# Perceiver block, expert slots: rows read six slots ahead and ahead of the weights; latent weights queued after the gathered rows

## The chip, the core and the metric

The kernel runs on one core of one Trainium2 chip. The metric is device time in microseconds (us) of that core. Three runs of the kernel before gave 1575.37, 1575.95 and 1579.69 us; the median is 1575.95 us.

## What is computed

Eight batches of 64 latent rows of 512 (512 rows in all) pass through two layers; each attends to a context of 8 x 1601 x 512. Everything is float32. Cut to what matters here:

```python
x = x + cross_attention_16_heads(layernorm(x), ctx, ...)        # layer 0
x = x + gated_scan(layernorm(x), ...)
x = x + ffn(layernorm(x), router_w, router_b, expert_w, expert_b)
#   ffn: each row goes to the one expert of 8 with the largest probability:
#   y = gate * (row @ expert_w[idx] + expert_b[idx])
x = x + cross_attention_1_head(ctx, ctx, layernorm(x), ...)     # layer 1
x = x + latent_attention(layernorm(x), Wq, Wl, Wk, Wv, Wo, ...)
x = x + encoder_layer_with_moe(layernorm(x), ..., w1, w2, ...)
```

The change touches the expert ffn of layer 0 and the loading of the weights of latent_attention (Wq 512x512, Wl 512x128, Wk and Wv 128x512, Wo 512x512) in layer 1.

## The kernel before, in words

**Layer 0 and routing.** The 512 rows lie in four tiles of 128. A tile is routed (`route_tile`, `places`), and its normalised rows are scattered to an array in DRAM, `xsd`, by an indirect transfer that GpSimd issues (L985). `xsd` has 11 slots of 128 rows (E + MORE = 8 + 3): one for each expert, and three that are given to experts with more than 128 rows.

**Expert slots** (`slots()`, L1127 to L1189). For each slot s, the rows `xs[s]` are read from `xsd` (`rows`, L1145, 256 KB), TensorE turns them (`turn`, L1149 and L239, result `xsT`), eight matmul instructions multiply them by the expert weights `ws[s]` (`fetch`, L1136 or, for the slots 8 to 10, an indirect transfer issued by GpSimd at L1139; 1 MB), VectorE copies the result to `ys` (L1165), and it is written to `ysd` in DRAM (L1166, 256 KB). Weights have four buffers (WE = 4), so the weights of slot s + 4 are asked for when slot s has been multiplied; before the change the rows of slot s + 4 are asked for just after them. Slot s + 2 is turned after slot s is multiplied. At slot 6 the third piece of the context of the first two batches is asked for as well (`context(0, 2)`, L1247, four tiles of 512 KB).

After slot 10, GpSimd gathers each token's row out of `ysd` (tiles `g`, L1180, four transfers of 256 KB), VectorE adds it to x (L1182) and normalises (L104 to L109, with two steps on GpSimd at L98 and L99), TensorE turns the result and makes the queries of the layer 1 attention (`queries1`).

**Layer 1.** `scores1` multiplies queries by the transposed context (tiles `w` from `ctxT`, bank `psc`), `attend1` multiplies probabilities by the context (tiles `w` from `ctx`, bank `pa`), both for pairs of batches bp = 0 to 3, in chunks c = 0 to 2 of four tiles of 512 KB each and a short tail. These tiles come out of a ring of 14 buffers (`ring_tile`): a tile can be asked for when TensorE is through with the one 14 before it. `latent_weights()` (L1290), called by the first `attend1`, asks for the five transfers of the latent weights (L1293: `lwq` 1 MB, `wl` 256 KB, two halves of `wkv` 256 KB each, `lwo` 1 MB) and six rows of biases (L1079). `latent(t)` uses them later. The last stage, the encoder layer with its own experts, streams 64 MB of weights (`w1`, `w2`).

**What sets the order.** Nearly all loads and stores are issued by SyncE (SP), one after another in a fixed order: one that has to wait holds up all that are behind it. An SP transfer can wait for a buffer, for the data that it reads, and for one of eight earlier transfers to land, so that at most eight are in flight. TensorE's order is written out in the program (`interleave`, and a manual schedule). For SP the order is written out by hand up to the end of `slots()` (`in_order.close()`, L1186); behind that a scheduler places the transfers, and `tc.keep_in_program_order` keeps a step from being moved ahead of where the program has it.

Of the kernel before, what the change touches and what calls it, by code (L numbers as in the profile page):

```python
# [16 lines left out]
NT = 4  # L17
DC = 4
SK = 1601
E, FF, CAP = 8, 2048, 64  # L20
WE = 4
MORE = 3
SLOTS = E + MORE
CH = [(0, 512), (512, 512), (1024, 512), (1536, 65)]
# [21 lines left out]
def perceiver_kernel(ctx: ExitStack, tc: tile.TileContext, a: dict, out: bass.AP):  # L46
    nc = tc.nc
# [7 lines left out]
    def name(s):  # L55
        count[0] += 1
        return f"{s}_{count[0]}"

    def ps(tag, shape=(128, 512), bufs=None):
        n = name(tag)  # L60
        return pools["psum"].tile(list(shape), F32, tag=tag, name=n, bufs=bufs)
# [39 lines left out]
    def layer_norm(dst, src, g=None, b=None):  # L101

        st = sm([128, 6], "ln_st")
        nc.vector.bn_stats(st, src)  # L104
        mv = sm([128, 2], "ln_mv")
        nc.vector.bn_aggr(mv, st)
        rs = sm([128, 1], "ln_rs")
        rsqrt(rs, mv[:, 1:2])
        nc.vector.tensor_scalar(dst, src, mv[:, 0:1], rs, ALU.subtract, ALU.mult)  # L109
        if g is not None:  # L110
            nc.vector.tensor_mul(dst, dst, g)
            nc.vector.tensor_add(dst, dst, b)
# [120 lines left out]
    def mm(p, w, m, start=True, stop=True, share=1.0):  # L233
        nc.tensor.matmul(p, w, m, start=start, stop=stop)  # L234
        n = m.free_size()
        clock[0] += share * max(2 * 0.85 * n, 230.0)
# [121 lines left out]
    posi = small.tile([128, NT], mybir.dt.int32, tag="posi", name="posi", bufs=1)  # L358
    wrow = small.tile([128, MORE], mybir.dt.int32, tag="wrow", name="wrow", bufs=1)
    xsd, ysd = [tc.dram_tile((SLOTS * 128, D), F32, name=nm) for nm in ("xsd", "ysd")]  # L360


    with ExitStack() as st:
# [588 lines left out]
        def places():  # L952
# [31 lines left out]
            for t in range(NT):  # L984
# [6 lines left out]

            past = work[:, 128 : 128 + MORE * E].rearrange("p (s e) -> p s e", e=E)
            nc.vector.tensor_tensor(
                past, upto.unsqueeze(1).to_broadcast([128, MORE, E]),
                iota0[:, :MORE].unsqueeze(2).to_broadcast([128, MORE, E]), ALU.is_le,
            )
            whose = work[:, 256 : 256 + MORE]
            nc.vector.reduce_sum(whose, past, axis=AX.X)
# [70 lines left out]
    routed = ctx.enter_context(ExitStack())  # L1069
    we = routed.enter_context(tc.tile_pool(name="we", bufs=WE, reuse_waits="tile"))  # L1070

# [5 lines left out]
    def row(nm, pool=None, bufs=3):  # L1077
        r = (pool or md).tile([128, D], F32, tag="row", name=name("row"), bufs=bufs)
        nc.sync.dma_start(r, a["rows"][ROWS.index(nm)].partition_broadcast(128))  # L1079
        return r  # L1080
# [4 lines left out]
    def t2(nm):  # L1085
        return md.tile([128, D], F32, tag="t2", name=name(nm), bufs=14)
# [27 lines left out]
    def flip_tile(v):  # L1114
        p = ps("pt")
        for c in range(DC):
            flip(p[:, ts(c, 128)], v[:, ts(c, 128)])
        return p
# [4 lines left out]
    x_mid = [Event() for _ in range(NT)]  # L1123
    x_out = [Event() for _ in range(NT)]
    xns, probs1 = {}, {}

    def slots():  # L1127


        ws, xs, xsT = first_ws, {}, {}  # L1130

        def fetch(s):
            if s < E:
                if s > 1:
                    ws[s] = we_tile(s)
                nc.sync.dma_start(ws[s], table[ts(s, 128), :])  # L1136
            else:
                ws[s] = we_tile(s)
                nc.gpsimd.indirect_dma_start(  # L1139
                    ws[s], None, table, bass.IndirectOffsetOnAxis(ap=wrow[:, s - E : s - E + 1], axis=0)  # L1140
                )

        def rows(s):
            xs[s] = t2("xs")
            nc.sync.dma_start(xs[s], xsd[ts(s, 128), :])  # L1145

        def turn(s):
            xsT[s] = t2("xsT")
            nc.scalar.copy(xsT[s], flip_tile(xs[s]))  # L1149

        rows(0)
        rows(1)
        for s in range(2, 4):
            fetch(s)
            rows(s)
        yield 13000.0
        for s in range(2):
            turn(s)
            yield 0.0
        for s in range(SLOTS):  # L1160
            p = ps("pp")
            for c in range(DC):
                mm(p, xsT[s][:, ts(c, 128)], ws[s][:, ts(c, D)], c == 0, c == 3)
            y = t2("ys")
            nc.vector.tensor_copy(y, p)  # L1165
            nc.sync.dma_start(ysd[ts(s, 128), :], y)  # L1166
            if s + WE < SLOTS:
                fetch(s + WE)
            if s + 4 < SLOTS:
                rows(s + 4)  # L1170
            if s + 2 < SLOTS:
                turn(s + 2)
            if s == 6:

                sooner[0, 2] = context(0, 2)
            yield 0.0
        slotted.set()
        gs = [t2("g") for _ in range(NT)]
        for t in range(NT):
            nc.gpsimd.indirect_dma_start(gs[t], None, ysd, bass.IndirectOffsetOnAxis(ap=posi[:, t : t + 1], axis=0))  # L1180
        for t in range(NT):
            nc.vector.scalar_tensor_tensor(x[:, t, :], gs[t], gates[:, t : t + 1], x[:, t, :], ALU.mult, ALU.add)  # L1182
            xns[t] = t2("xn")
            layer_norm(xns[t], x[:, t, :])
            x_in[t].set(6500.0 + NORM + 1.5 * t * COPY)
        in_order.close()  # L1186
        routed.close()
        nonlocal ml
        ml = latents.enter_context(tc.tile_pool(name="ml", bufs=2, reuse_waits="tile"))  # L1189
# [51 lines left out]
    def context(bp, c):  # L1241
        kts = []
        for h in range(2):
            k = []
            for j in range(2):
                kt = ring_tile()
                nc.sync.dma_start(  # L1247
                    kt, a["ctxT"][2 * bp + h, ts(j, 256), ts(c, 512)].rearrange("(c p) s -> p c s", p=128)
                )
                k += split(kt)  # L1250
            kts.append(k)
        return kts
# [37 lines left out]
    def latent_weights():  # L1290

        def late(dst, src):
            tc.keep_in_program_order(nc.sync.dma_start(dst, src))  # L1293

        for k, n, tag in (("q", "Wq", "lwq"), ("l", "Wl", "wl"), ("o", "Wo", "lwo")):
            v = a["L1_attn_" + n]
            lw[k] = ml.tile([128, DC, v.shape[1]], F32, tag=tag, name=tag, bufs=1)
            if n != "Wo":
                late(lw[k], v.rearrange("(c p) e -> p c e", p=128))
        lw["kv"] = ml.tile([128, 2, D], F32, tag="wkv", name="wkv", bufs=1)  # L1300
        late(lw["kv"][:, 0, :], a["L1_attn_Wk"])
        late(lw["kv"][:, 1, :], a["L1_attn_Wv"])
        late(lw["o"], a["L1_attn_Wo"].rearrange("(c p) e -> p c e", p=128))
        lw["bo"], lw["bv"], lw["b2"] = [row(n, ml) for n in ("L1_attn_bo", "L1_attn_bv", "L1_ffn_ln2_b")]
        mh["ob"], mh["g1"], mh["b1"] = [row("L1_ffn_" + n) for n in ("out_proj_b", "ln1_g", "ln1_b")]

        m16 = md.tile([128, 16], F32, tag="m16", name="m16", bufs=1)
        tc.keep_in_program_order(nc.vector.reduce_sum(m16, ident.rearrange("p (b c) -> p c b", c=16), axis=AX.X))
        nc.vector.tensor_scalar(m16, m16, -1.0, 1e30, ALU.add, ALU.mult)
        mh["mask"] = md.tile([128, 128], F32, tag="mask", name="mask", bufs=1)  # L1310
        nc.vector.tensor_copy(
            mh["mask"].rearrange("p (b c) -> p b c", c=16), m16.unsqueeze(1).to_broadcast([128, 8, 16])
        )

    lw = {}
# [26 lines left out]
    def attend1(bp):  # L1342
# [4 lines left out]
        if bp == 0:  # L1347
            latent_weights()
# [285 lines left out]
    def we_tile(s):  # L1634

        return we.tile([128, DC * D], F32, tag=f"we{s % WE}", name=name("we"), bufs=1)

# [9 lines left out]
    for c in range(2):  # L1647
# [6 lines left out]
        + [(-9, mha_turn()), (-8, first_turns())]  # L1654
        + [(0.5 * t - 2.5, queries1(t)) for t in range(NT)]
        + [(30, slots()), (31, expert_bias()), (32, fold_vo()), (40, mha())]
    )

# [267 lines left out]
```

## Time and profile before

| | us |
|---|---|
| median of three runs | 1575.95 |
| the profiled execution's own time | 1579.39 |
| its span, first to last instruction | 1577.6 |
| TensorE busy (97% of the span) | 1523.0 |
| VectorE busy | 737.6 |
| expert slots on TensorE, first turn to last multiplication | 1047.3 to 1097.1 |
| gathers of `g` issued / rows turned for the queries | 1100.9 to 1104.6 / 1112.6 |
| first scores of layer 1 | 1125.9 |
| encoder weights stream without a gap | about 1420 to 1550 |

In the profile, times in a timeline count from the span's start. A line of a timeline gives start, duration, engine, line of the code, operation, output and inputs, and the number of instructions merged; brackets give the idle time of the engine before it and what ended it. Matrix multiplications in float32 show as two instructions each, and the end of a multiplication is modelled, so consecutive rows overlap a little. A table of windows gives for each stretch its length, the busy time of each engine with the number of instructions, the clock granted to TensorE (1.00 is full), the mean busy share of the 16 DMA engines (about 1.05 when they have no gap), and GB/s moved.

### The profile page before, as it was taken

The numbers are of one execution on the slowest core, as the hardware profiler recorded it, in microseconds if no ns is written. First come the engines' busy times: TensorE is split into PE (matmuls) and PEld (weight loads), VectorE is DVE, ScalarE is ACT, GpSimd is POOL, SyncE is SP. The second block draws the span as 40 slices with busy tenths as digits, with TensorE's granted clock in tenths as the row PEclk, the third lists the DMA queues.
The fourth block names the chain that finished last, engine by engine and source line by source line (L and its number), as shares of the span: only waits on it lengthen the run. The fifth ranks groups of instructions, "written<-read, shape, count | busy, mean of one in ns | idle before, by whom it ended". The sixth has DMA issues, their size and how long they took to land. (4 is left out here: it accounts for less than half of the span.)

```text
span 1577.6 us, 23169 instructions
## 1 busy us (share of the span) xinstructions
PE 1523.0 (97%) x9446; PEld 1127.0 (71%) x9446; DVE 737.6 (47%) x1743; ACT 298.4 (19%) x539; POOL 220.5 (14%) x265
## 2 busy tenths in 40 slices
PE   7999999999999999999999999998899998999997
PEld 6788888878888888888888888754544556664432
DVE  6255554555564555555555666421322344351113
ACT  0122222122122222222222222111001111200000
POOL 5211111111110111211021000011200121110000
PEclk9999999999999999999999999989899999989999
DMA  8211111021111111111111401568799840719995
GB/s 238 52 41 28 34 28 27 28 54 34 28 27 28 27 54 35 28 28 27 42 40 27 139 1 40 220 219 294 271 373 366 298 160 1 261 67 378 374 376 218
DMA packets 129739, 197.67 MB, mean 125 GB/s; under 512 B 27856, under 2 KB 54224, under 8 KB 128224
## 3 DMA queue, kind: packets, MB, share of 16 engines
q1 hardware_dynamic: 128560, 190.93, 36.4%
q0 software_dynamic: 1072, 5.24, 0.9%
q8 instruction: 75, 1.23, 0.3%
q14 instruction: 32, 0.26, 0.1%
HBM read 188.28 MB, written 7.86 MB: 124 GB/s over the span
## 5 line engine op out<-in xcount | busy, mean ns | idle before, releaser
L472 PE MATMUL bk<-pc,Tk 128*128 128x256 f32 x768 | 176.1, 383 | 3.6 <-POOL pc L409 3.6
L516 PE MATMUL bk<-Tv,pc 128*128 128x256 f32 x768 | 175.3, 379 | 0.0
L472 PEld LDWEIGHTS bk<-pc,Tk 128*128 128x128 f32 x768 | 146.4, 191 | 24.4 <-POOL pc L409 4.0
L516 PEld LDWEIGHTS bk<-Tv,pc 128*128 128x128 f32 x768 | 144.0, 190 | 19.9 <-issue 1.4
L472 PE MATMUL bk<-pc,k 128*128 128x256 f32 x576 | 137.1, 384 | 4.4 <-DMA pc<-in_ctxT_dram 4.4
L516 PE MATMUL bk<-v,pc 128*128 128x256 f32 x576 | 134.5, 381 | 0.0
L585 DVE TENSOR_SCALAR_CACHE_REDUCE s<-bk 128x512 f32<-128x512 f32 (+1 forms) x227 | 125.3, 615 | 15.0 <-PE bk L234 15.0
L621 ACT ACTIVATE s<-s,sx_nm 128x1601 f32<-128x1601 f32 x64 | 103.8, 1624 | 147.5 <-DVE sx_nm L618 147.5
L472 PEld LDWEIGHTS bk<-pc,k 128*128 128x128 f32 x576 | 107.9, 192 | 18.8 <-DMA k<-in_L_xattn_Wk_dram 4.4
L516 PEld LDWEIGHTS bk<-v,pc 128*128 128x128 f32 x576 | 107.4, 190 | 14.3
L239 PE MATMUL bk<-ident,s 128*128 128x128 f32 (+1 forms) x832 | 103.3, 273 | 0.0
L239 PEld LDWEIGHTS bk<-ident,s 128*128 128x128 f32 (+1 forms) x832 | 94.1, 141 | 9.5 <-PE bk L234 1.5
L499 DVE TENSOR_TENSOR kT<-bk,tm 128x512 f32<-128x512 f32 x96 | 65.1, 690 | 67.0 <-PE bk L472 65.1
L649 ACT COPY pT<-bk 128x512 f32<-128x512 f32 x96 | 56.1, 585 | 213.0 <-PE bk L239 212.2
L532 DVE TENSOR_TENSOR vU<-bk,tm 128x512 f32<-128x512 f32 x96 | 66.0, 691 | 60.5 <-PE bk L516 58.5
L408 POOL TENSOR_TENSOR pc<-pc,pc 128x512 f32<-128x512 f32 x24 | 30.4, 1267 | 452.7 <-PE bk L516 290.3
L234 PE MATMUL pa<-pT,vU 128*64 128x128 f32 x1536 | 92.7, 275 | 0.0
L234 PE MATMUL bk<-kT,qbd 64*128 64x512 f32 x384 | 91.9, 608 | 0.0
L234 PEld LDWEIGHTS pa<-pT,vU 128*64 128x64 f32 x1536 | 83.0, 137 | 10.0 <-issue 8.8
L651 DVE COPY pT<-bk 128x512 f32<-128x512 f32 x96 | 65.5, 686 | 33.6 <-PE bk L239 33.4
L528 DVE TENSOR_TENSOR tm<-bk,tm 128x512 f32<-128x512 f32 x72 | 49.4, 687 | 44.2 <-PE bk L516 43.3
L98 POOL TENSOR_SCALAR ln_rs<-ln_mv 128x1 f32<-128x1 f32 x32 | 10.7, 334 | 417.3 <-DVE ln_mv L1671 194.4
(329 smaller groups left out, 1923.6 us busy)
## 6 DMA issues: line engine op xcount, KB each, us to landing
w<-in_L_ffn_w_dram SPq DMA_DIRECT2D x128, 512.0 KB, 10.6
pc<-in_ctxT_dram SPq DMA_DIRECT2D x96, 256.0 KB, 2.8
w<-in_ctxT_dram SPq DMA_DIRECT2D x48, 512.0 KB, 10.1
w<-in_ctx_dram SPq DMA_DIRECT2D x48, 512.0 KB, 9.7
we<-in_L_ffn_expert_w_dram SPq DMA_DIRECT2D x8, 1024.0 KB, 7.1
pc<-in_L_xattn_Wo_dram SPq DMA_DIRECT2D x12, 256.0 KB, 2.5
w<-in_L_ffn_in_proj_w_dram SPq DMA_DIRECT2D x6, 512.0 KB, 9.2
xsd<-zero SPq DMA_DIRECT2D x11, 256.0 KB, 3.6
```

What stands on the lines that cost most here:

```text
L234: nc.tensor.matmul(p, w, m, start=start, stop=stop)
L239: nc.tensor.transpose(p, v, ident)
L408: nc.gpsimd.tensor_add(S[0], A[1, 0], A[1, 1])
L472: nc.tensor.matmul(p[:, ts(e, 256)], Wk[i][:, d, ts(e, 128)], A[i][:, d, :], start=(d == 0), stop=(d == 1))
L499: nc.vector.tensor_add(o[:, 2 * j : 2 * j + 2, ts(i, 256)], p.rearrange("p (e s) -> p e s", e=2), s.rearrange("p (e s) -> p e s", e=2),)
L516: nc.tensor.matmul(p[:, ts(k, 256)], A[i][:, d, ts(k, 128)], Wv[i][:, d, :], start=(d == 0), stop=(d == 1))
L528: nc.vector.tensor_add(t, p, s)
L532: nc.vector.tensor_add(o[i][:, :, ts(j, 256)], p.rearrange("p (k e) -> p k e", k=2), s.rearrange("p (k e) -> p k e", k=2))
L585: nc.vector.tensor_scalar(s[i][:, c0 : c0 + n], p, 1.0, None, ALU.mult, ALU.max, accum_out=mx[:, i, c0 // 512 : c0 // 512 + 1],)
L621: nc.scalar.activation(s[i], s[i], AF.Exp, bias=nm[:, i : i + 1], scale=scale, accum_out=rs[:, i : i + 1])
L649: nc.scalar.copy(o, v)
L651: nc.vector.tensor_copy(o, v)
```

## The change

Three edits. (1) The rows of six slots instead of four are asked for before the slot loop (`AHEAD = 6`), the first four of them ahead of the weights of slots 2 and 3; in the loop, the rows of slot s + 6 are asked for ahead of the weights of slot s + 4. (2) The list `gs` of gathered tiles is made visible outside `slots()`. (3) In `latent_weights()`, VectorE copies one column of the first gathered tile into `lwq` ahead of the load of `lwq`; this keeps that load, and the four that are kept in program order behind it, from being issued before the gathered rows are there.

```diff
+AHEAD = 6
...
+    gs = []
...
-        rows(0)
-        rows(1)
-        for s in range(2, 4):
-            fetch(s)
+        for s in range(4):
+            rows(s)
+        fetch(2)
+        fetch(3)
+        for s in range(4, AHEAD):
             rows(s)
...
             nc.sync.dma_start(ysd[ts(s, 128), :], y)
+
+            if s + AHEAD < SLOTS:
+                rows(s + AHEAD)
             if s + WE < SLOTS:
                 fetch(s + WE)
-            if s + 4 < SLOTS:
-                rows(s + 4)
...
-        gs = [t2("g") for _ in range(NT)]
+        gs.extend(t2("g") for _ in range(NT))
...
             lw[k] = ml.tile([128, DC, v.shape[1]], F32, tag=tag, name=tag, bufs=1)
+            if k == "q":
+
+                tc.keep_in_program_order(nc.vector.tensor_copy(lw[k][:, 0, 0:1], gs[0][:, 0:1]))
             if n != "Wo":
                 late(lw[k], v.rearrange("(c p) e -> p c e", p=128))
```

In the built programs the order of instructions on TensorE, ScalarE and GpSimd is the same before and after. VectorE has one more, the copy; it stands between the second L170 of layer 1 and L1308. On SP, the rows move as told above, and the five loads of latent weights move from between the context tails (L1267) and the next two context tiles to behind 20 context tiles: the twelve of `ctxT` for bp = 1 and the first eight of `ctx` for bp = 0. The rest of `ctx` for bp = 0 and all later tiles stand behind them.

## The prediction

> **What bounds the kernel now.** TensorE is busy for 97% of the span, so I first asked where it waits around the change. The table of TensorE's waits from 1045 to 1250 us (total, times, longest) has five waits that matter:
>
> ```profile
> PE pt L239 <- DMA xs<-xsd: 5.4, 6, 1.8
> PE pt L239 <- DVE xn L109: 5.1, 1, 5.1
> PE pt L239 <- DVE ln_mv L106: 2.1, 1, 2.1
> PE pa L234 <- DMA w<-in_ctx_dram: 0.8, 1, 0.8
> PE psc L234 <- DMA w<-in_ctxT_dram: 0.7, 1, 0.7
> ```
>
> The first is what the new order of rows is about. The second and third stand behind the gathers, which is what the later latent weights are about. The last two are small, but they say that in layer 1 TensorE is just caught up with the transfers. So I read the windows there, for the DMA share (second number from the end):
>
> ```profile
> 1100.00:1110.00 10.00, 7.46 (x27) 4.73 (x25) 2.16 (x4) 0.75 (x2) 3.79 (x4) 1.00 1.02 329
> 1110.00:1120.00 10.00, 5.30 (x24) 4.96 (x25) 7.45 (x15) 1.17 (x2) 5.66 (x10) 0.53 0.77 283
> 1120.00:1130.00 10.00, 10.00 (x70) 7.27 (x70) 1.76 (x3) 0.00 (x0) 3.42 (x3) 0.96 0.18 41
> 1130.00:1140.00 10.00, 10.00 (x62) 3.85 (x60) 2.34 (x11) 2.21 (x3) 0.00 (x0) 1.00 1.02 380
> 1160.00:1170.00 10.00, 10.00 (x48) 3.60 (x45) 0.75 (x1) 0.85 (x2) 0.00 (x0) 1.00 1.05 357
> 1200.00:1210.00 10.00, 9.26 (x51) 4.57 (x48) 1.45 (x3) 1.54 (x3) 0.00 (x0) 1.00 1.05 387
> ```
>
> The latent weights fill 1100 to 1117; then the DMA engines are nearly idle (0.18), because the next context tiles wait for buffers that the first scores (1125.9) set free; from 1130 to 1250 there is no gap. What is asked for in the idle stretch is free; what is asked for after 1130 pushes everything behind it. SP's timeline shows what is in front of and behind the gathers (GpSimd issues those at 1100.85 to 1104.61):
>
> ```profile
> 1097.88 0.32 SPq L1166 DMA_DIRECT2D ysd<-ys  x1
> ...
> 1099.94 0.45 SPq L1293 DMA_DIRECT2D lwq<-in_L_attn_Wq_dram  x1
> 1100.44 0.51 SPq L1293 DMA_DIRECT2D wl<-in_L_attn_Wl_dram  x1
> 1101.00 0.49 SPq L1293 DMA_DIRECT2D wkv<-in_L_attn_Wk_dram  x1
> 1101.54 0.86 SPq L1293 DMA_DIRECT2D wkv<-in_L_attn_Wv_dram  x1
> ...
> 1107.92 0.47 SPq L1293 DMA_DIRECT2D lwo<-in_L_attn_Wo_dram  x1
> 1108.44 15.33 SPq L1079 DMA_DIRECT2D row<-in_rows_dram  x4
> 1127.86 2.08 SPq L1247 DMA_DIRECT2D w<-in_ctxT_dram  x3
> ```
>
> **Part 1, rows ahead.** In TensorE's timeline a slot that waits for nothing takes 3.87 us (multiplications at 1052.59 and 1056.46), the last two take 7.03 together. Unhindered, the slots would end at 1048.62 + 3.97 + 8 x 3.87 + 7.03 = 1090.6 instead of 1097.1: at most 6.5 us. The rows no longer wait behind 1 MB of weights. The weights now wait behind 256 KB of rows (0.65 us by the landings of rows and weights in the trace). Weights took 7.1 to 9.2 us to land; with 0.65 more that fits into the three slots (11.6 us) between asking and use. But a slot moves 1.5 MB, some 4.1 us at 387 GB/s and 4.6 us by the landings between 1062 and 1080, against 3.87 us of TensorE, so a backlog grows, and the weights of slots 9 and 10 may come some 1 us late. I take 5.5 us (bounds 1.5, if slots run at nearly the pace of the landings, and 6.5). The six early rows cost nothing: 0.5 MB more is 1.3 us, and the DMA engines stand idle from 1051 to 1053.
>
> **Part 2, gathers without the latent weights in front.** The first gather took 7.35 us (issued 1100.85, landed 1108.20; `lwq` landed at 1107.00), all four 6.9 to 7.35. Nearest free transfers: the scatter to `xsd`, 2.7 us, and the last store to `ysd`, 2.07 us. In front of them are left the context tails and now three bias rows (768 KB, 2 us), so I put the first landing at about 1104.1 in the time of before, 4.1 us earlier. TensorE works on the folding of weights until 1107.5; the first turned row then comes 4.3 us after the landing, as before, at 1108.4 instead of 1112.5. A rule of the Trainium skill speaks against this gain: by "DMA: Bandwidth & Descriptors", section "Queues, rings and completion order", each DMA engine takes turns between the queues that have work. The gathers are on GpSimd's queue, the latent weights on SP's, so by the rule a gather would get half of 387 GB/s, 1.35 us for its 256 KB after some 2.7 us of latency, about 4.1 us even before, and there would be at most 1 us to gain. The row has 7.35 us and a landing just behind `lwq`, so I go with the row. A store backlog from the faster slots takes back 0.4: 3.7 us (bounds 0.8 and 5). The clock fell to 0.5 from 1110.6 to 1120.8, after 3.2 us of idleness; in the changed kernel TensorE idles 1 us and then 2.7 us for the second row. Whether that keeps the clock up no row tells: -2.5 to +2.5 us, taken as nothing, as the gap is split and not gone.
>
> **Part 3, where the latent weights go.** They move into the stretch without a gap, behind 20 context tiles and in front of chunk 2 of `ctx` for bp = 0. That is 2.88 MB, 7.45 us at 387 GB/s (a 512 KB tile lands every 1.355 us there). They also wait for VectorE's copy of one column (0.15 us of VectorE, as for the 128x4 copy at L1028, beside other work). It stands behind the second L170 in VectorE's order:
>
> ```profile
> 1155.56 0.16 DVE L170 RECIPROCAL sx_rr<-sx_rs 128x1 f32<-128x1 f32 x1 [2.02 <-ACT s L168]
> 1155.64 0.35 DVE L1308 TENSOR_REDUCE m<-ident 128x16 f32<-128x128 f32 x1
> ```
>
> So it comes 29.7 us after the first scores (1125.9). SP has issued the eighth `ctx` tile 22.9 us after them (1148.8) and then stands for 6.9 us; queued behind it are all later tiles, for which TensorE waits. The tiles in flight cover most of this: the eighth landed at 1156.5, and a tile issued to idle engines lands after 4.1 us (the first, at 1127.86), so the gap is about 1.7 us. Together 9.2 us later. TensorE needs the third tile of chunk 2 at 1161.66 and it landed at 1161.39: slack 0.3 us. So TensorE stalls there by some 8.5 us, and since it was waiting for transfers again up to 1204 (the 0.8 and 0.7 above; the tiles land there just as they are used), it does not make this up: **8.9 us lost** (bounds 7.2, bytes only, and 11, if the clock falls during the stall). After 1204 tiles land 5 to 10 us before use, so nothing is added. The latent weights themselves are in time: first used at 1207.7.
>
> **The sum.** -5.5 - 3.7 + 8.9 = -0.3 us, on the profiled execution's 1579.4 (span 1577.6 and 1.8 around it), 3.4 above the median of the runs. The later stages, ordered by TensorE and then fed by weights whose buffers come free when layer 1 ends, move along. Taken from the median: 1575.95 - 0.3 = 1575.7.
>
> **Rivals.**
> *The gains hold and the insertion is cheaper (0.22).* Slots at 6.5, gathers at 5 with the clock kept at 1.00 (2), against 7.2 for the bytes: -6.3, about 1569.6. For it: the stretch before the scores is full of waits that hang on the gathers. Against: every tile from 1164 to 1215 lands 1.355 us after the one before, so bytes put in there cannot hide.
> *Slower: the slots are bound by bytes, not by the order of rows (0.26).* Rows asked sooner then only move the wait from `xs` to `we`. Place: the slots from 1060 on. Price: part 1 gives 0.5 instead of 5.5, so -0.5 - 3.7 + 8.9 = +4.7, and about +5 with the 0.3 to 0.5 us that the weights lose to rows put ahead of them: 1581. It decides if a slot's 1.5 MB take over 4.4 us; the landings have 4.6. Against: the share there is 0.92 to 0.97, not 1.05, and weights landed 4 us or more before use.
> *The change does not do what it says:* the gathers are as slow with the bias rows, tails and the store backlog in front; then part 2 gives 0.8, +2.6, 1578.5; it counts into no change.
>
> **How the numbers follow.** Likeliest, 0.52: gains and loss cancel, 1571 to 1580. About 0.3%, 4.7 us, is what a measurement of this kernel can tell from no change: faster 0.22, same 0.52, slower 0.26. The range of 8 in 10 reaches into both rivals: 1569 to 1582.5.
>
> **What would show it.** Right: the waits for `xs` gone, slots ending near 1091.5; gathers landing in about 4 us, first scores about 1116.5; then one new wait of TensorE of some 8.5 us at L234 `pa` on `in_ctx`, about 36 us after the first scores, SP standing before L1293 for 7 us, and the end of layer 1 where it was. Wrong: no such wait (then the kernel is faster by up to 9 us), waits for `we` in the slots, gathers still at 7 us, or a clock of 0.5 for long after the new stall.

## The result, and the profile after

The changed kernel takes 1580.51 us (median of 20 runs, 1576.71 to 1583.1), the kernel before 1577.67 (20 runs beside it). The ratio is 1.0019, 95% interval 1.0011 to 1.0028: about 3.0 us slower, where the forecast was 0.3 faster. The profiled execution took 1579.66 us, span 1577.9. Each part acted where it was said to act, but the sizes were off, and they don't cancel.

TensorE's waits from 1045 to 1250 us, after the change:

```profile
PE pa L235 <- DMA w<-in_ctx_dram: 7.4, 3, 6.1
PE pt L240 <- DVE xn L110: 3.3, 1, 3.3
PE pt L240 <- DVE ln_mv L107: 2.6, 1, 2.6
PE psc L235 <- DMA w<-in_ctxT_dram: 0.6, 1, 0.6
```

The 5.4 us for `xs` are gone, those behind the gathers fell from 7.2 to 5.9, and the wait for context went from 0.8 to 7.4. (The line numbers have moved by 1 from line 23 on, and by 2 to 7 behind line 1126.) TensorE's timeline shows the new wait in one place, chunk 2 of `ctx` for bp = 0, as forecast:

```profile
1148.41 3.65 PE L235 MATMUL pa<-w,pT 128*64 128x512 f32 x16
1152.00 0.33 PE L240 MATMUL pt<-ident,s 128*65 128x128 f32 x1
1158.45 1.94 PE L235 MATMUL pa<-w,pT 128*64 128x512 f32 x2 [6.13 <-DMA w<-in_ctx_dram]
1161.07 7.08 PE L235 MATMUL pa<-w,pT 128*64 128x512 f32 x18 [0.68 <-DMA w<-in_ctx_dram]
```

SP's timeline shows what now stands in front of the gathers (GpSimd issues them at 1093.10 to 1096.86), and where the latent weights went:

```profile
1090.41 1.59 SPq L1271 DMA_DIRECT2D ct<-in_ctxT_dram  x3
1092.06 1.45 SPq L1080 DMA_DIRECT2D row<-in_rows_dram  x3
1097.94 2.10 SPq L1251 DMA_DIRECT2D w<-in_ctxT_dram  x2
...
1127.45 12.33 SPq L1368 DMA_DIRECT2D w<-in_ctx_dram  x8
1146.41 0.37 SPq L1297 DMA_DIRECT2D lwq<-in_L_attn_Wq_dram  x1
```

The three bias rows (768 KB) have moved up into the place of `lwq`, in front of the gathers. After the eighth `ctx` tile SP issues nothing until 1146.41. In SP's table of waits that is one line; it names the instruction behind the one that SP waited for, which VectorE's timeline shows, the pinned copy (L1304; pinned means written with `tc.keep_in_program_order`):

```profile
SPq L1297 <- DVE m L1315: 6.8, 1, 6.8
```

```profile
1146.15 0.16 DVE L171 RECIPROCAL sx_rr<-sx_rs 128x1 f32<-128x1 f32 x1 [2.02 <-ACT s L169]
1146.23 0.15 DVE L1304 COPY lwq<-g 128x1 f32<-128x1 f32 x1
```

The windows of the same stretch (busy time of each engine, TensorE's clock, DMA share, GB/s):

```profile
1100.00:1110.00 10.00, 4.46 (x22) 4.29 (x23) 7.61 (x16) 1.17 (x2) 5.28 (x10) 0.74 0.34 116
1110.00:1120.00 10.00, 10.00 (x70) 7.59 (x70) 1.61 (x3) 0.00 (x0) 3.81 (x3) 0.92 0.14 32
...
1140.00:1150.00 10.00, 10.00 (x66) 4.32 (x64) 3.52 (x15) 2.21 (x3) 0.00 (x0) 1.00 0.73 261
1150.00:1160.00 10.00, 3.87 (x13) 0.85 (x9) 0.00 (x0) 0.26 (x1) 0.00 (x0) 0.80 1.05 377
1160.00:1170.00 10.00, 9.32 (x29) 2.82 (x30) 0.75 (x1) 0.59 (x1) 0.00 (x0) 0.69 1.05 363
```

The DMA engines are now mostly idle from 1100 to 1120 (0.34 and 0.14), where the latent weights used to come for nothing. They also lose 3 us between 1140 and 1150 (0.73 where 1.05 is full): SP stood longer than the tiles in flight could bridge. Then the DMA engines have no gap, and TensorE waits.

**Stages.** Slot 0 starts anywhere from 1046.65 to 1049.21 us in the profiles of this case, and at 1046.65 and 1048.05 in two profiles of one and the same kernel. So I compare lengths of stages from slot 0 on, each read from the start of a multiplication in TensorE's timeline (us). Where the trace doesn't tell when a gather landed, the start of the first addition of a gathered row stands for it. The last three rows repeat kernels or are controls (experiment 5); two profiles of one kernel differ by up to 0.7.

| kernel | slots | slots' end to first scores | first scores to latent stage | first gather, issue to landing |
|---|---|---|---|---|
| before | 48.3 | 28.9 | 81.8 | 7.35 |
| changed | 41.8 | 27.4 | 92.3 | 5.48 |
| rows only | 41.8 | 28.3 | 81.6 | 6.94 |
| latent weights only | 47.1 | 26.6 | 92.5 | 5.76 |
| early wait | 41.8 | 27.7 | 81.8 | 5.72 |
| same place, no wait | 41.8 | 27.5 | 89.1 | 5.02 |
| wait without the bytes | 41.8 | 28.4 | 84.9 | 6.73 |
| bias rows behind | 41.8 | 25.2 | 81.2 | 3.24 |
| nothing in front | 41.8 | 24.2 | 85.2 | 3.33 |
| four slots ahead | 47.2 | 29.4 | 81.8 | 8.04 |
| wait without the bytes, again | 41.8 | 28.5 | 85.1 | 7.4 |
| rows only, again | 41.8 | 28.9 | 81.2 | 7.5 |
| no stand | 41.9 | 28.7 | 81.2 | 7.5 |

For the change this reads -6.5 - 1.5 + 10.5 = +2.5 us; the medians have +3.0. In the two profiled executions alone it is hidden (+0.3), as slot 0 came 1.3 us earlier in the one of after, and the later stages were some 0.8 shorter.

### The profile page after: what moved, and what is told of

It is laid out like the page before. It is cut to its first block, busy times and chain, and to the rows that moved or that the text cites. A ratio compares the mean times of both kernels' runs of the same rounds, so it can differ in the third digit from the quotient of the medians.

```text
span 1577.9 us, 23167 instructions
## 1 busy us (share of the span) xinstructions
PE 1525.6 (97%) x9446; PEld 1129.2 (72%) x9446; DVE 736.5 (47%) x1744; ACT 298.8 (19%) x539; POOL 220.7 (14%) x265
```

## The experiments

My theory after the result: the gain of the slots is whole, the latent weights cost their bytes where they now stand plus a wait of SP, and the gathers gain little because other bytes took the place in front of them. The rivals: SP's stand is paid in full, or costs nothing; and, for the gathers, what is in front of them doesn't matter.

**1. Rows only.** The changed kernel without the copy, so that the latent weights are again asked for in front of the gathers.

```diff
-            if k == "q":
-                tc.keep_in_program_order(nc.vector.tensor_copy(lw[k][:, 0, 0:1], gs[0][:, 0:1]))
```

> The changed kernel without the copy and its wait: rows six slots ahead, latent weights asked for where they were before. Bytes theory (the latent weights cost their bytes wherever the stream has no gap): the slots keep the whole 6.5 us, the gathers land after 7 us again, no stall of TensorE at the third chunk of ctx, so 5 to 6.5 us below the kernel before. Rival (the rows give nothing in the end because the stream of layer 1 sets the pace whatever starts it): within 2 us of before.

Measured: 1569.27 us beside 1576.7 of before, ratio 0.9950 (0.9936 to 0.9963). TensorE's waits:

```profile
PE pt L240 <- DVE xn L110: 4.8, 1, 4.8
PE pt L240 <- DVE ln_mv L107: 2.1, 1, 2.1
PE psc L235 <- DMA w<-in_ctxT_dram: 0.3, 1, 0.3
...
PE pa L235 <- DMA w<-in_ctx_dram: 0.2, 1, 0.2
```

No wait for `xs` and none worth the name for `ctx`. The rows alone give 5.5 to 8 us (another run of it is in experiment 5), where 5 to 6.5 were expected; everything that the change loses comes from moving the latent weights.

**2. Latent weights only.** The kernel before with the copy.

```diff
+            if k == "q":
+                tc.keep_in_program_order(nc.vector.tensor_copy(lw[k][:, 0, 0:1], gs[0][:, 0:1]))
```

> The kernel before with only the copy and its wait added. If the parts simply add up, it is the changed kernel's +2.8 us plus the 6.5 us of the rows: 8 to 10 us above before. If the stall absorbs whatever is gained ahead of it (rival), it is only some 3 us above before.

Measured: 1587.91 us, ratio 1.0071 (1.0057 to 1.0084), with both waits in TensorE's table:

```profile
PE pa L234 <- DMA w<-in_ctx_dram: 7.8, 4, 6.0
PE pt L239 <- DMA xs<-xsd: 4.3, 5, 1.8
```

That is 11 us above before (9 to 13), where 8 to 10 were expected. The two halves add up to the whole: -0.0050 + 0.0071 = +0.0021, measured +0.0019.

**3. Early wait.** The copy stays but isn't pinned; VectorE then does it right behind the first addition of a gathered row, and the latent weights come in the idle stretch before the first scores.

```diff
-                tc.keep_in_program_order(nc.vector.tensor_copy(lw[k][:, 0, 0:1], gs[0][:, 0:1]))
+                nc.vector.tensor_copy(lw[k][:, 0, 0:1], gs[0][:, 0:1])
```

> The changed kernel with the copy left free to be placed: it then stands just behind the first gathered row in VectorE's order, and SP asks for the latent weights in the stretch in which the DMA engines are idle, ahead of the context tiles that wait for the first scores. Bytes theory: no stall, slots -6.5, gathers -1.6, some +0.5 for the copy and a reduction in front of the normalisation: 7 to 8 us below before. Rival (any wait of SP on VectorE costs the stream its length): no gain over before.

Measured: 1570.33 us, ratio 0.9960 (0.9947 to 0.9974). The stretch from the first scores to the latent stage is back at 81.8 us. So it is the place that costs, not the dependence on a gathered row. But the gain is 6.3 us and not the 7 to 8 expected, and no more than rows only gives: of the gathers' 1.2 us (5.72 for 6.94) the first scores gain 0.6.

**4. Same place, no wait.** The five loads are written where the changed kernel has them, behind the eighth `ctx` tile, with no copy in front. Only the place of the call is shown; the loads themselves move out of `latent_weights()` into `late_loads()`.

```diff
...
             pT, cts = nxt, load(c)
+            if bp == 0 and c == 1:
+                late_loads()
...
```

> The latent weights at the very place in SP's order that they have in the changed kernel, without the copy, so that SP does not stand. Bytes theory: only the gap of some 1.5 to 2 us goes, so 1 to 2.5 us below the changed kernel, about +0.5 to +1.5 against before. Wait theory (the 6.8 us in which SP stands are the cost): 6 us or more below before.

Measured: 1576.07 us, ratio 1.0000 (0.9992 to 1.0008), and in TensorE's waits

```profile
PE pa L235 <- DMA w<-in_ctx_dram: 5.8, 2, 4.4
```

From the first scores to the latent stage it takes 89.1 us, 7.5 over rows only: the 7.45 us that 2.88 MB take at 387 GB/s. With the wait (changed kernel, latent weights only) it is 92.3 and 92.5, so the wait adds 3.3. By the ratios, bytes are 0.0050, or 7.9 us, and the wait 0.0019, or 3.0 us: a little over the 1 to 2.5 expected for the gap, and half of what the wait theory asks for.

**5. The wait without the bytes**, and two controls. Latent weights in front of the gathers, but the pinned copy at the changed kernel's place, and behind it a load of one column (128x1) again. Only the added lines are shown; the changed kernel's copy is taken out.

```diff
+        tc.keep_in_program_order(nc.vector.tensor_copy(lw["q"][:, 0, 0:1], gs[0][:, 0:1]))
+        late(lw["q"][:, 0, 0:1], a["L1_attn_Wq"][0:128, 0:1])
```

> The rows-only kernel (latent weights back in front of the gathers), with one column of a gathered row copied into the latent query weight at the place of the changed kernel's copy, and a 128x1 column asked for again behind that copy on SyncE's queue. It issues the changed kernel's wait without its 2.88 MB. Theory (the stream of context tiles is gap-free, so what counts is bytes, and the stand of SP costs only what the transfers already asked for don't bridge): the rows-only kernel's ratio of 0.995 plus about 3 us, 4 to 5 us under the kernel before (ratio 0.997), with a wait of TensorE for `pa` of about 2.5 us. Rival 1 (the stand of SP is paid in full, 7 us): level with the kernel before, ratio 0.9995. Rival 2 (the stand costs nothing, and the 10.5 us that the changed kernel loses behind the first scores are bytes and the lower clock): ratio 0.995, no wait of TensorE.

Measured: 1575.29 us, ratio 0.9988 (0.9978 to 0.9999): some 6 us over rows only, though its profile has 3.3 more. This interval alone doesn't exclude rival 1. SP's waits show the same stand as the changed kernel; TensorE's wait for `pa` is 1.6 us in three pieces where some 2.5 in one were expected:

```profile
SPq L1297 <- DVE m L1314: 6.9, 1, 6.9
```

```profile
PE pa L235 <- DMA w<-in_ctx_dram: 1.6, 3, 0.7
PE psc L235 <- DMA w<-in_ctxT_dram: 1.2, 2, 0.6
```

3.3 against 6 us was open, and the two kernels had not run side by side. So the wait ran again beside rows only, with a third kernel that has the same copy and small load, the copy not pinned, so that nothing stands.

> The kernel with the wait and without the bytes once more, now beside the rows-only kernel on one chip. Its profile showed 3.3 us more than the rows-only kernel between the first scores and the latent stage, the medians of two calls 6 us more. If the profile's 3.3 us are all, the two ratios of this call differ by 0.002; if a lower granted clock adds to it in most executions, by 0.004, and the mean clock of this kernel's runs is below that of the rows-only kernel by 0.002 or more.

> The rows-only kernel once more, as the base of the two others of this call: ratio 0.995 by both theories, mean granted clock 0.988.

> The kernel with the wait and without the bytes, its copy not pinned: the same 128x1 copy and the same 128x1 load, but early, where SyncE doesn't stand. If the stand of SyncE is all that the wait costs, this is level with the rows-only kernel: ratio 0.995, no wait of TensorE for `pa`. If the copy or the small load itself costs something, it keeps part of the loss, 0.996 to 0.999.

Measured: wait again 1574.43 us, ratio 0.9985 (0.9976 to 0.9993); rows only again 1570.24, 0.9965 (0.9949 to 0.9981); no stand 1569.21, 0.9956 (0.9940 to 0.9972). From the first scores to the latent stage: 85.1, 81.2 and 81.2 us. The copy and the small load cost nothing that can be seen. The stand costs 3.3 to 3.9 us by the stages; by the ratios 0.0020 over rows only and 0.0029 over no stand, or 3.2 and 4.6 us; and by the means of the times measured side by side 3.9 us, 95% interval 2.7 to 5.1 (21 runs with the wait, 12 of the two kernels without). That leaves out both rivals, nothing and 6.9 us; the 6 us of the first comparison can be scatter. The windows show where it is lost, first with the wait (the first of its two profiles), then rows only again:

```profile
1145.00:1155.00 10.00, 10.00 (x65) 4.16 (x61) 3.38 (x13) 2.20 (x3) 0.00 (x0) 1.00 0.66 237
```

```profile
1145.00:1155.00 10.00, 10.00 (x65) 4.16 (x63) 3.28 (x12) 2.47 (x4) 0.00 (x0) 1.00 1.05 360
```

A share of 0.66 where 1.05 is full means 3.7 us of idle DMA engines (3.2 in the second profile, with 0.71): what the stand is worth beyond the tiles in flight. The mean granted clock is the same (0.987) with the wait and without, so a lower clock is not part of it.

**6. What is in front of the gathers.** The early wait with the three bias rows behind the latent weights too; then also the first two context tails made to wait for the gathered row.

```diff
-        lw["bo"], lw["bv"], lw["b2"] = [row(n, ml) for n in ("L1_attn_bo", "L1_attn_bv", "L1_ffn_ln2_b")]
+        for k, n in (("bo", "L1_attn_bo"), ("bv", "L1_attn_bv"), ("b2", "L1_ffn_ln2_b")):
+            lw[k] = ml.tile([128, D], F32, tag="row", name=name("row"), bufs=3)
+            late(lw[k], a["rows"][ROWS.index(n)].partition_broadcast(128))
```

> The kernel with the early wait (copy not pinned, ratio 0.996), with the three bias rows of the latent attention asked for behind the latent weights too, so that only three context tails stand in front of the gathers. If the gathers wait for the bytes in front of them on SyncE's queue, their first landing comes 3.5 to 4 us after the request where it took 5.5 in the changed kernel, first scores come about 1.5 to 2 us earlier, and the ratio falls to about 0.995. Rival: 5.5 us is the gather's own time and the rows in front of it cost nothing; landing at 5 to 5.5 us, ratio 0.996.

```diff
+                if bp < 2:
+                    nc.vector.tensor_copy(kt[:, 0, 0, 0:1], gs[0][:, 0:1])
+                    nc.vector.tensor_copy(kt[:, 1, 0, 0:1], gs[0][:, 0:1])
```

> The last kernel with the two early context tiles made to wait for the first gathered row as well: nothing of SyncE's queue stands in front of the gathers. If bytes in front count, the first gather takes 2.5 to 3.5 us; if 5.5 us is its own time, it still takes 5 or more. The context then lands later than it does now, so that a wait of TensorE at `pa` or `psc` may take back what the gathers gain: from 3 us below the kernel before to 3 us above it, ratio 0.998 to 1.002. The landing is what this run is for.

Measured: bias rows behind 1565.79 us, ratio 0.9933 (0.9919 to 0.9946), the fastest of all, 10.6 us under the kernel before. Nothing in front: 1569.44, 0.9950 (0.9937 to 0.9962), outside the 0.998 to 1.002 expected. The view of the tile `g` gives the time from issue to landing over the four gathers; first the changed kernel:

```profile
L1184 POOL DMA_INDIRECT g<-ysd,posi x4: 946/948/951, 1093.1 to 1096.9; - x4
DMA to landing us min/median/max: 4.3/5.2/5.6
```

with the bias rows behind:

```profile
L1184 POOL DMA_INDIRECT g<-ysd,posi x4: 946/950/1073, 1092.5 to 1096.2; - x4
DMA to landing us min/median/max: 3.2/3.6/6.8
```

The first gather by itself takes 3.2 to 3.3 us; with 768 KB in front, which is 2.0 us at 387 GB/s, 5.0 to 5.8; with `lwq` and more in front, 6.7 to 8.0. So the first gather pays for what SP has asked for before it and what hasn't landed. But the longest, 6.8, is the fourth: GpSimd's instruction for it started 0.4 us before SP issued `lwq`, took 1.07 us, and the rows came 0.9 us before `lwq` did. So a load asked for at nearly the same time likely delays a gather too. Taking the tails away as well does nothing for the first landing (3.3), but the fourth then lands after 4.7 us and not 6.8, and the first scores come 1.0 us earlier. It costs 4 us behind the first scores: the bias rows, asked for from 1125.76 in the full stream, are 2.0 us of bytes at 387 GB/s; the rest was not taken apart.

**7. Four slots ahead.** Rows only, with the rows in front of the weights but the distance as before.

```diff
-AHEAD = 6
+AHEAD = 4
```

> The rows-only kernel with rows asked for four slots ahead as before, but in front of the weights. If the order on the queue is what makes slots wait for `xs`, all of the 6.5 us that the slots gained are kept: ratio 0.995, no wait for `xs`. If it is the distance (six slots instead of four), nothing is kept: the rows then still stand behind the context tile and the weights of the slots before, slots end where they ended, ratio 0.9995. I expect about half, since in front of slots 8 to 10 no weights are left to pass on that queue and only the early requests pass the context tile: ratio 0.997, waits for `xs` of about 2 us.

Measured: 1577.17 us, ratio 0.9998 (0.9988 to 1.0009): nothing is kept, where I had expected half. TensorE's timeline has one long wait in place of six short ones (5.4 us together before):

```profile
1078.34 1.09 PE L240 MATMUL pt<-ident,xs 128*128 128x128 f32 x4 [3.72 <-DMA xs<-xsd]
```

These are the rows of slot 8: asked for at 1068.02, landed at 1078.21, while TensorE wanted them at 1074.6. In the changed kernel they were asked for two slots earlier, at 1059.87, and landed at 1065.22. So the gain needs the distance, and the place in front of the weights alone doesn't give it: in this stretch a 256 KB read was 10 us on its way, and four slots of distance leave 6.6 us. What holds it up is likely GpSimd's 1 MB of weights for slot 8, asked for 0.3 us before (at 1067.68) and landed at 1076.67; no run takes these away. The order alone did shorten the waits, from 5.4 to 3.7 us, but in the one long wait the clock fell to half for 3.4 us (1077.9 to 1081.3), and the multiplications behind it took some 1.7 us longer. So the slots are 1.1 us shorter than before and 5.4 longer than with six slots ahead. Six slots ahead but behind the weights was not run. Beyond the slots this run's other stages are as those of rows only within about a microsecond.

## Why the prediction was wrong

The signs that the prediction listed came, but for the gathers: no waits for `xs`, SP standing for 6.8 us, one new stall of `pa` where it was put. First scores at 1116.49 (forecast 1116.5) are luck: slot 0 started 1.3 us earlier and the slots gained 1.0 us more, which made up for the gathers. What failed is the size of two terms, the gathers' landing (part 2, 2.2 us too large a gain) and the gap behind SP's stand (part 3, 1.6 us too small a loss); part 1 was 1.0 us too low. From -0.3 that makes +2.5.

- **Part 1 (-5.5 us) measured -6.5**, the upper bound. The weights of slots 9 and 10 were not late; no wait for `we` appears. The rival "bound by bytes" is out for the distance of six, and for four it is nearer than the prediction had it: order alone gathered most of the wait in one slot (experiment 7). The prediction's reason, that rows no longer wait behind 1 MB of weights, was thus only a part of it.
- **Part 2 (-3.7 us) measured -1.5** (-1.2 to -2.3 in the four kernels with the bias rows in front). The step that failed is "so I put the first landing at about 1104.1": this leaves 3.25 us between issue and landing, with 2 us of bias rows in front. But 3.2 to 3.3 us is what a gather takes with none of them in front (experiment 6); with them it took 5.48, which is 1.9 earlier than before and not 4.1. The prediction named the rows and their 2 us and then didn't add them: its own figures, 2.7 us for a free transfer and 2 for the rows, give 4.7. The -3.7 us would have been right for the kernel with the bias rows moved too: there the landing is 4.1 us earlier and the stretch shrank by 3.8. Part of this is the clock, which the prediction took as nothing: it was at half for 10.2 us behind the gathers before, for 6.8 in the changed kernel and for 3.4 with the bias rows moved. The Trainium skill's rule of turns between queues ("DMA: Bandwidth & Descriptors", section "Queues, rings and completion order") left at most 1 us to gain, on the prediction's estimate that turns mean half the rate; the page has turns by packets and says nothing of half. Against the two profiles of rows only, the change gained 1.5 and 2.0 us of landing and 0.9 and 1.5 at the first scores, so that size came closer than my reading, by luck: by it the gather would have landed after some 4.1 us with any load on SP's queue, where it took 3.2 to 8.0 with what stood in front. That doesn't refute turns; equal halves don't fit. The row's reading, that SP's bytes delay the gather, holds, and was misapplied.
- **Part 3 (+8.9 us) measured +10.5.** The bytes were right (7.45 forecast, 7.5 in experiment 4). The gap was put at 1.7 us and less 0.3 of slack; it measured 2.8 in the landings and 3.3 to 3.9 in experiments 4 and 5. In the landings: the eighth `ctx` tile came at 1146.60 and `lwq` at 1152.07, where without a gap its 1 MB would have ended at 1146.60 + 2.71 = 1149.31. Three things make the 1.1 us. The prediction's own figures give 1.95 and not 1.7 (1148.8 + 6.9 + 4.1, less 1156.5 and 1.355). The tiles in flight covered 0.6 less than assumed: the eighth landed 0.2 us after SP issued again, where 0.8 was assumed (it took 7.2 us from its issue, 7.7 before). And the restart took 2.95 us over `lwq`'s own bytes (5.66 to its landing less 2.71), where the 4.1 us of a smaller tile are 2.75 over its 1.355. Bytes and gap make 10.3 of the 10.5; TensorE didn't make up any of it, as forecast.
- **The clock** fell to half in the new stall, from 1156.0 to 1166.3, which the prediction listed as a risk of up to 2 us. It cost nothing that can be seen by the latent stage: TensorE waited for tiles again at 1199.7 and 1204.7 (0.6 us each), and the DMA engines had no gap between (1.05), so the tiles set the end of the stretch. The kernel with the wait and no bytes, whose two profiles have no such stretch there, pays the same for the wait.

Open stays the half microsecond from the stages' +2.5 to the medians' +3.0, which is within their interval (1.7 to 4.4).

## What to carry to other kernels

A load moved out of the way of an urgent transfer should land in a stretch where the DMA engines idle; here the same five loads cost 7.5 us more in the full stream some 50 us later and nothing in the idle stretch, and one wait in front of them on a queue that feeds everything cost 3 to 4 more. Ask what moves up into the vacant place: here the bias rows did. With the rows six slots ahead, the early wait and the bias rows moved too, the kernel was 0.67% (0.54 to 0.81) faster than before. When requests are early by a number of steps, compare that time with the time of flight in that stretch (10 us here, where a transfer of this size with nothing in front takes 2 to 3); here a change of the order alone left 3.7 of 5.4 us of waiting.

## What the runs showed of the hardware

- A gather issued by GpSimd was held up by bytes that SP had asked for before it: the first took 3.2 to 3.3 us without, 5.0 to 5.8 with 768 KB, 6.7 to 8.0 with the latent weights in front. A queue of its own didn't protect it. The gather that a 1 MB load of SP followed within 0.4 us took 6.8 us.
- When nearly all transfers had landed, the next 1 MB landed 5.66 us after its issue, 2.95 over its own bytes at 387 GB/s; a stand of SP of 6.8 us behind eight tiles in flight left a gap of 2.8 us.
- In a stall of TensorE of 6.1 us the clock fell to half after 3.7 us and stayed there for 10.2; in a stretch bound by transfers this had no price that can be seen. At the 3.7 us wait of experiment 7 it fell for 3.4 us, and there it cost some 1.7.
